# More identity transposes ahead of the weight product, later bias columns and row, and stores of z from two queues in a two-layer graph kernel

## Chip, cores and metric

The kernel runs on one core of one Trainium2 chip. The metric is device time in microseconds (us). Before the change three runs gave 1083.54, 1084.51 and 1085.01 us, so the median is 1084.51 us.

## What is computed

x has 32 batches of 512 rows and 512 columns in float32; adj is a 512 x 512 matrix: the edges of a random graph and a full diagonal, with random weights. Two layers follow each other, each with a layer norm and a relu ahead of it and a residual around it:

```python
h = jnp.maximum(_layernorm(x, axis=-1), 0.0)
x = x + einsum('nm,bmd->bnd', adj, h) @ weight + bias
h = jnp.maximum(_layernorm(x, axis=-1), 0.0)
# attention with q, k, v = h @ Wq + bq, h @ Wk + bk, h @ Wv + bv, 8 heads
scores = q @ k.T / sqrt(64) + (1.0 - adj) * -1000000000.0
x = x + softmax(scores) @ v @ Wo + bo
```

The mask term is so large that each row's softmax is one at the largest entry of its row of adj and zero elsewhere. So layer 1 is, for the inputs at hand, a gather: row n takes h of its one column, times Wv @ Wo, plus the constant row bv @ Wo + bo. A flag that the kernel computes from the data says whether this holds; then the function `single_path` runs, otherwise another that is not used here.

## The kernel before, in words

There are two stages. **The first stage**, the body of `gnn_two_layers` up to line 268, prepares what does not depend on the batch, and batch 0. It is written out in the order in which each engine shall work (a manual schedule: an engine executes its instructions in the order of the program text). On TensorE it runs, in this order:

- 14 transposes of the identity matrix (line 140), which need no loaded data, into a PSUM tile that nothing reads;
- `turn(0)`, the transposes of the first chunk of Wv (line 116), copied to `wvT` by ScalarE (line 117);
- the product Wv @ Wo (line 148) in four groups i of four matmuls; `turn(1)` to `turn(3)` stand between them, and the transposes of adj (line 106) after groups 1 and 2;
- the aggregation of batch 0 (line 225) in four groups d, with a few small matmuls between them: column counts (232), sums over partitions (218, 219), the broadcast of the row bv @ Wo (224), and the verdict of all partitions (221).

VectorE in the meantime finds the largest entry of each row of the mask (`peaks`), the layer-norm statistics (`norms`), sums of operand blocks for a seven-product scheme of 2 x 2 block multiplication (`sum_a`, `sum_b`), and then the verdict (`decide`) and the flag (line 255). The four `bias_part` steps (lines 133 and 135) form bv * Wo on VectorE, one chunk each, from the column tile `bv_c`. GpSimd computes the reciprocal standard deviations (`power`, line 326) and issues the small loads: `bv_c`, and the columns of bq and bk (`bt`), at the start (line 98), and the rows b0 and bo in the middle (line 162). ScalarE evacuates PSUM, applies the relus, and sums the squares of bq, Wq, bk and Wk (`squares`, lines 199 and 200).

Every engine then loads the flag (line 270) and branches (line 271). **The second stage**, `single_path`, runs over the batches with a table of steps: in each batch b, pieces of VectorE, ScalarE, GpSimd and DMA work are put (`put(batch, step, f)`) into 21 slots beside the 21 block products of TensorE (line 388), and batch 0 has a plain form of layer 0 (line 514). Layer 1 of a batch makes a compact z, which VectorE transposes (line 593), which is stored to DRAM by four DMAs for each part (line 598), and gathered from there back into the rows by GpSimd DMAs (`finish`, and `fetch` for the last batches, line 611). There are two parts of z in a batch: chunks 0 to 5 and chunks 6 to 10.

At the end, the batch before the last (B - 2) ends its layer 1 while batch B - 1 takes a plain form: its h rows are gathered (line 545), transposed (`transpose_all`, line 552), copied by ScalarE (553) and multiplied (`layer1_rows`, line 564), with the adds of the gathered z of batches B - 3 and B - 2 (`add_z`, line 616) and the last stores (lines 567 and 617) between the four row groups.

Of the kernel before, what the change touches and what calls it, by code (L numbers as in the profile page):

```python
# [17 lines left out]
P = 128  # L18
# [7 lines left out]
def gnn_two_layers(ctx: ExitStack, tc: tile.TileContext, x, adj, w0, b0, wq, bq, wk, bk, wv, bv, wo, bo, out):  # L26
# [15 lines left out]
    nc = tc.nc  # L42
    B, N, D = x.shape
    C = N // P
    DC = D // P
# [7 lines left out]
    adjT, yT, w0_s, sel, wvo = big("adjT"), big("yT"), big("w0_s"), big("sel"), big("wvo")  # L53
    adjT_s, w0_t, wvo_t = (keep.tile([P, 4, 2, N // 2], F32, name=n) for n in ("adjT_s", "w0_t", "wvo_t"))
    wv_s, wo_s = xs[3], xs[4]
    cvo = keep.tile([P, D], F32, name="cvo")
# [6 lines left out]
    ident = keep.tile([P, P], F32, name="ident")  # L63
# [8 lines left out]
    with ExitStack() as tmp, tc.manual_schedule():  # L72
# [6 lines left out]
        bt = [look.tile([P, DC], F32, name=f"bt{i}") for i in range(2)]  # L79
        bv_c = look.tile([P, DC], F32, name="bv_c")  # L80
# [13 lines left out]
        make_identity(nc, ident)  # L94
        nc.gpsimd.memset(ones, 1.0)
        nc.gpsimd.memset(mhalf, -0.5)
        for t, v in ((bv_c, bv), (bt[0], bq), (bt[1], bk)):
            nc.gpsimd.dma_start(t, v.rearrange("(c p) -> p c", p=P))
        first = look.tile([P, 1], F32, name="first")
        nc.scalar.activation(first, ones[:, 0:1], AF.Relu)  # L100

# [11 lines left out]
        def turn(i):  # L113
            pt = ps_l.tile([P, C, P], F32, name=f"pt{i}")
            for j in range(DC):
                nc.tensor.transpose(pt[:, j, :], wv_s[:, i, j * P:(j + 1) * P], ident)  # L116
            (nc.scalar.copy, nc.scalar.copy, nc.vector.tensor_copy, nc.vector.tensor_copy)[i](
                wvT[:, :, i * P:(i + 1) * P], pt)
# [12 lines left out]
        def bias_part(j):  # L131
            if j == 0:
                nc.vector.tensor_scalar_mul(part, wo_s[:, 0, :], bv_c[:, 0:1])
            else:
                nc.vector.scalar_tensor_tensor(part, wo_s[:, j, :], bv_c[:, j:j + 1], part, op0=ALU.mult, op1=ALU.add)

        flips = transposed(adj_s, adjT)
        idle = ps_l.tile([P, C, P], F32, name="pt3")
        for i in range(14):
            nc.tensor.transpose(idle[:, i % C, :], ident, ident)  # L140
        turn(0)
        later = {(0, 2): 1, (1, 0): 2, (1, 2): 3}
        for i in range(DC):
            ps = ps_l.tile([P, D], F32, name="mm", bufs=2)
            for j in range(DC):
                if (i, j) in later:
                    turn(later[i, j])
                nc.tensor.matmul(ps, wvT[:, j, i * P:(i + 1) * P], wo_s[:, j, :], start=(j == 0), stop=(j == DC - 1))  # L148
            if i == 0:
                for j in range(DC):  # L150
                    bias_part(j)
            if i == 1:
                next(flips)
                peaks(0)
                peaks(1)
            if i == 2:
                next(flips)
                for n in (0, 1):
                    norms[0].stats(n)
                norms[0].power()  # L160
                for v, r in ((b0, b0_r), (bo, cvo)):
                    nc.gpsimd.dma_start(r, bass.AP(tensor=v.tensor, offset=v.offset, ap=[[0, P], [1, D]]))
                norms[1].stats(0)
                norms[0].offset()
                norms[1].stats(1)
                norms[1].power()
            nc.scalar.copy(wvo[:, i, :].rearrange("p (c q e) -> p q c e", q=4, c=4),
                           ps.rearrange("p (q c e) -> p q c e", q=4, c=4))
            if i < 2:
                scale(2 * i)  # L170
                scale(2 * i + 1)
            if i == 2:
                next(flips)
                norms[0].relu(0)
                norms[0].relu(1)
                peaks(2)
                norms[1].offset()
                peaks(3)
                norms[1].relu(0)
                norms[1].relu(1)  # L180
# [8 lines left out]
        nc.vector.tensor_reduce(least, gap, AX.X, ALU.min)  # L189
        for i in range(4):  # L190
            sum_b(nc, adjT_s, adjT, i)

        sums = look.tile([P, 4], F32, name="sums")
        few = ps_l.tile([P, 4, C], F32, name="few")
# [19 lines left out]
        for d in range(DC):  # L214
            ps = ps_l.tile([P, N], F32, name="mm", bufs=2)
            for m in range(C):
                if d == 2 and m == 1:
                    nc.tensor.matmul(many[:, 0, :], ones, used, start=True, stop=True)
                    nc.tensor.matmul(many[:, 1, :], ones, sums, start=True, stop=True)
                if d == 3 and m == 2:  # L220
                    nc.tensor.matmul(few[0:1, 1, 0:1], sure, ones[:, 0:1], start=True, stop=True)
                if d == 3 and m == 0:
                    bias = ps_l.tile([P, D], F32, name="pt0")
                    nc.tensor.matmul(bias, ones, part, start=True, stop=True)
                nc.tensor.matmul(ps, hs[0][:, m, d * P:(d + 1) * P], adjT[:, m, :], start=(m == 0), stop=(m == C - 1))  # L225
            if d == 0:
                squares(0)
            nc.scalar.copy(yT[:, d, 0:N // 2 if d == 3 else N], ps[:, 0:N // 2 if d == 3 else N])
            if d == 0:
                squares(1)  # L230
                for m in range(C):
                    nc.tensor.matmul(few[:, 0, m:m + 1], both[:, m * P:(m + 1) * P], ones[:, 0:1],
                                     start=True, stop=True)
                if B > 1:
                    norms.append(Norm(nc, small, mhalf, xs[1], hs[1], range(C)))
                    norms[2].stats(0)
                nc.vector.tensor_scalar_min(used, few[:, 0, :], 1.0)
                if B > 1:
                    for c in range(1, C):
                        norms[2].stats(c)  # L240
                    norms[2].power()
                for i in range(2):
                    sum_b(nc, w0_t, w0_s, i)
                if B > 1:
                    norms[2].offset()
            if d == 2:
                decide()
                nc.vector.memset(before[:, 0:1], 0.0)
                for m in range(1, C + 1):
                    nc.vector.tensor_add(before[:, m:m + 1], before[:, m - 1:m], many[:, 0, m - 1:m])  # L250
                for c in (0, 1):
                    nc.vector.max_index(idx[:, c, :], top[:, c, :], mask[:, c, :])
                for i in range(3):
                    sum_a(nc, wvo_t, wvo, i)
        nc.vector.tensor_copy(flag, few[0:1, 1, 0:1])
        for c in (2, 3):
            nc.vector.max_index(idx[:, c, :], top[:, c, :], mask[:, c, :])
        nc.vector.tensor_copy(yT[:, 3, N // 2:N], ps[:, N // 2:N])
        nc.vector.tensor_add(cvo, bias, cvo)
        nc.vector.tensor_mul(part.rearrange("p (c q e) -> p c q e", q=4, c=4),  # L260
                             cvo.rearrange("p (q c e) -> p c q e", q=4, c=4),
                             ident.rearrange("p (q e) -> p q e", q=4).unsqueeze(1).broadcast_to([P, 4, 4, 32]))
# [33 lines left out]
def sum_b(nc, s, t, i, half=256):  # L296
    b11, b12, b21, b22 = blk(t, 0, 0, half), blk(t, 0, 1, half), blk(t, 1, 0, half), blk(t, 1, 1, half)
    if i == 0:
        nc.vector.tensor_sub(s[:, 0], b12, b11)
    elif i == 1:  # L300
        nc.vector.tensor_sub(s[:, 1], b22, s[:, 0])
    elif i == 2:
        nc.vector.tensor_sub(s[:, 2], b22, b12)
    else:
        nc.vector.tensor_sub(s[:, 3], b21, s[:, 1])
# [36 lines left out]
def single_path(ctx: ExitStack, tc: tile.TileContext, x, wv, bv, wo, bo, out, kept, room):  # L342
# [15 lines left out]
    nc = tc.nc  # L358
# [190 lines left out]
    def transpose_all(r):  # L549
        pt = ps_t.tile([P, DC, P], F32, name="pt")  # L550
        for d in range(DC):
            nc.tensor.transpose(pt[:, d, :], hs[0][:, r, d * P:(d + 1) * P], ident)
        nc.scalar.copy(hs[1][:, :, r * P:(r + 1) * P], pt)
# [35 lines left out]
    def put_z(b, s0, s1):  # L589
        if b not in Z:  # L590
            Z[b] = dram.tile([32 * S, D], F32, name="z")
            ZR[b] = work.tile([P, S, P], F32, name="hc" if b == B - 2 else "zr")
        nc.vector.transpose(ZR[b][:, s0:s1, :].rearrange("p s (c e) -> p s c e", c=4),
                            ZT[b][:, :, 32 * s0:32 * s1].rearrange("p c (s j) -> p s c j", j=32))
        rows = Z[b].rearrange("(s j) (q f) -> q j s f", j=32, q=4)
        for q in range(4):
            eng = nc.scalar if q > 1 and (b, s0) == (B - 2, 0) else nc.sync
            eng.dma_start(rows[q][:, s0:s1, :], ZR[b][32 * q:32 * q + 32, s0:s1, :])

    def finish(b):  # L600
# [39 lines left out]
    with tc.manual_schedule():  # L640
        nc.gpsimd.affine_select(out=upper, in_=ones, compare_op=ALU.is_ge, fill=0.0, base=-1,
                                pattern=[[1, P]], channel_multiplier=-1)
        for b in range(B + 1):
            todo = [[] for _ in range(21)]

            def put(batch, step, f, *args):
                if 0 <= batch < B:
                    todo[step].append(lambda: f(batch, *args))
# [58 lines left out]
                todo[3] += todo[4] + todo[5] + todo[6]  # L707
                run(layer0_rows(0), todo[0:4])
            if b == B - 1:
                put(b, 18, lambda b: transpose_all(0))  # L710
            if b == 1:
                tables = []
                put(1, 0, lambda b: tables.append(places()))
# [270 lines left out]
```

## Time and profile before

| what | value |
|---|---|
| median of three runs | 1084.51 us |
| the profiled execution: its own time | 1083.92 us |
| the profiled execution: its span | 1081.7 us |
| TensorE matmul busy | 1067.9 us (99%) |
| VectorE busy | 902.8 us (83%) |
| ScalarE busy | 362.2 us (33%) |
| GpSimd busy | 439.2 us (41%) |
| TensorE waits of over 0.3 us | 1.43 us at the start, 0.68 us at 5.66, 1.72 us at 41.86, 1.37 us at 1054.16, 8.2 us after its last matmul at 1073.5 |

PE is TensorE's matmul row, PEld its weight loads, DVE is VectorE, ACT is ScalarE, POOL is GpSimd and SP is the engine that mostly issues DMAs; a q behind an engine's name is its sequencer. Times in the timeline are microseconds from the start of the span. One row of the timeline merges consecutive instructions of one kind: start, length, what, and in square brackets the idle time before it and what ended it. A float32 matmul of 512 columns leaves two records, a transpose of 128 columns one. The last record of a row is reported longer than its distance to the next one, so starts are the better measure.

### The profile page before, as it was taken

The numbers are of one execution on the slowest core, as the hardware profiler recorded it, in microseconds if no ns is written. First come the engines' busy times: TensorE is split into PE (matmuls) and PEld (weight loads), VectorE is DVE, ScalarE is ACT, GpSimd is POOL, SyncE is SP. The second block draws the span as 40 slices with busy tenths as digits, with TensorE's granted clock in tenths as the row PEclk, the third lists the DMA queues.
The fourth block names the chain that finished last, engine by engine and source line by source line (L and its number), as shares of the span: only waits on it lengthen the run. The fifth ranks groups of instructions, "written<-read, shape, count | busy, mean of one in ns | idle before, by whom it ended". The sixth has DMA issues, their size and how long they took to land.

```text
span 1081.7 us, 15914 instructions
## 1 busy us (share of the span) xinstructions
PE 1067.9 (99%) x5418; PEld 941.9 (87%) x5418; DVE 902.8 (83%) x1851; ACT 362.2 (33%) x664; POOL 439.2 (41%) x522
## 2 busy tenths in 40 slices
PE   9999999999999999999999999999999999999996
PEld 5488989999998999998999998999898899999893
DVE  5888888888888888888888988888888888888873
ACT  5324323334422324432323432323332333442331
POOL 2024554333454333454433354433455434355413
PEclk9999999999999999999999999999999999999998
DMA  9144766667767666767666776665766666775638
GB/s 329 40 96 141 183 183 160 160 167 196 187 179 181 151 167 184 196 176 188 150 160 183 201 185 175 160 167 158 207 183 183 146 169 171 196 186 151 148 104 265
DMA packets 162443, 186.90 MB, mean 173 GB/s; under 512 B 15024, under 2 KB 102320, under 8 KB 162352
## 3 DMA queue, kind: packets, MB, share of 16 engines
q1 hardware_dynamic: 132816, 116.89, 37.2%
q0 software_dynamic: 27968, 66.61, 26.8%
q10 hardware_dynamic: 1568, 2.29, 0.6%
q8 instruction: 44, 0.72, 0.3%
q14 instruction: 47, 0.39, 0.1%
HBM read 96.28 MB, written 89.46 MB: 172 GB/s over the span
## 4 chain that ended last, share of the span: by engine, by line
PE 94%; DMA 2%; DVE 1%; POOL 1%; issue 1%; ACT 1%; SPq 0%; POOLq 0%; ACTq 0%; DVEq 0%
PE mm L388 89%; PE mm L148 1%; PE mm L225 1%; PE mm L514 1%; POOL x L602 1%; DMA yT<-z,place 0%; ACT h L337 0%; DMA h<-hs,idx 0%; DMA z<-zr 0%; DMA out_dram<-x 0%; PE pt L140 0%; DMA hs<-h 0%; PE pt L116 0%; DVE st L319 0%; DVE x L616 0%
## 5 line engine op out<-in xcount | busy, mean ns | idle before, releaser
L602 POOL DMA_INDIRECT x<-z,place x116 | 182.7, 1575 | 351.8 <-issue 193.7
L427 ACT COPY yT<-mm 128x512 f32<-128x512 f32 x124 | 71.8, 579 | 542.6 <-PE mm L388 534.6
L445 DVE TENSOR_TENSOR x<-mm,x 128x512 f32<-128x512 f32 x217 | 149.6, 689 | 86.1 <-PE mm L388 86.1
L337 ACT ACTIVATE h<-x,off,rstd 128x512 f32<-128x512 f32 x256 | 194.3, 807 | 52.2 <-DVE off L329 49.9
L326 POOL TENSOR_TENSOR rstd<-ve,mhalf 128x2 f32<-128x2 f32 (+1 forms) x97 | 106.3, 1095 | 233.5 <-DVE ve L325 233.0
L319 DVE BATCH_NORM_STATS2 st<-x 128x6 f32<-128x512 f32 x256 | 171.4, 670 | 1.2
L388 PE MATMUL mm<-adjT_s,h0s 128*128 128x256 f32 x744 | 170.8, 379 | 0.2 <-ACT yT L427 0.2
L388 PE MATMUL mm<-w_t,sel 128*128 128x256 f32 x744 | 170.7, 379 | 0.0
L388 PEld LDWEIGHTS mm<-adjT_s,h0s 128*128 128x128 f32 x744 | 141.2, 190 | 19.9 <-ACT yT L427 0.6
L388 PEld LDWEIGHTS mm<-w_t,sel 128*128 128x128 f32 x744 | 141.3, 190 | 19.3
L526 POOL DMA_INDIRECT hs<-h,dest x124 | 126.7, 1022 | 23.9 <-issue 22.4
L388 PE MATMUL mm<-w_s,yT 128*128 128x256 f32 x496 | 117.2, 379 | 0.0
L388 PE MATMUL mm<-adjT,h 128*128 128x256 f32 x496 | 117.2, 379 | 0.0
L388 PE MATMUL mm<-hTs,wvo_t 128*128 128x168 f32 x720 | 112.4, 306 | 0.0
L438 ACT ACTIVATE zs<-mm,cvo_c 128x168 f32<-128x168 f32 x240 | 83.0, 397 | 75.5 <-PE mm L388 75.5
L388 PEld LDWEIGHTS mm<-adjT,h 128*128 128x128 f32 x496 | 94.2, 190 | 13.2 <-issue 0.5
L388 PEld LDWEIGHTS mm<-hTs,wvo_t 128*128 128x128 f32 x720 | 105.5, 190 | 0.0
L388 PEld LDWEIGHTS mm<-w_s,yT 128*128 128x128 f32 x496 | 92.9, 190 | 11.3
L494 DVE TENSOR_TENSOR x<-x,b_r 128x512 f32<-128x512 f32 x124 | 83.8, 676 | 0.0
L388 PE MATMUL mm<-hT,wvo 128*128 128x168 f32 x480 | 78.2, 306 | 0.0
L388 PEld LDWEIGHTS mm<-hT,wvo 128*128 128x128 f32 x480 | 72.7, 190 | 1.6
L425 DVE TENSOR_TENSOR yT<-mm,yT 128x512 f32<-128x512 f32 x93 | 64.0, 688 | 5.7 <-PE mm L388 1.7
(159 smaller groups left out, 1285.7 us busy)
## 6 DMA issues: line engine op xcount, KB each, us to landing
out_dram<-x SPq DMA_DIRECT2D x124, 256.0 KB
x<-in_x_dram SPq DMA_DIRECT2D x120, 256.0 KB
hc<-hs SPq DMA_DIRECT2D x124, 176.0 KB
z<-zr SPq DMA_DIRECT2D x120, 96.0 KB
z<-zr SPq DMA_DIRECT2D x120, 80.0 KB
hs<-h,dest POOLq DMA_INDIRECT x124, 6.3
x<-z,place POOLq DMA_INDIRECT x116
adj_s<-in_adj_dram SPq DMA_DIRECT2D x2, 512.0 KB
```

Of the source, the lines that this page charges most:

```text
L148: nc.tensor.matmul(ps, wvT[:, j, i * P:(i + 1) * P], wo_s[:, j, :], start=(j == 0), stop=(j == DC - 1))
L319: self.nc.vector.bn_stats(st, self.src[:, self.chunks[i], :])
L326: self.nc.gpsimd.tensor_tensor(self.rstd, ve, self.mhalf[:, 0:n], ALU.pow)
L337: self.nc.scalar.activation(dst, src, AF.Relu, bias=self.off[:, i:i + 1], scale=self.rstd[:, i:i + 1])
L388: nc.tensor.matmul(bank[:, m, 0:half], lhs[:, k, m * P:(m + 1) * P], rhs[:, k, :], start=(first and m == 0 and k == 0), stop=(k == 1), ski ...
L425: nc.vector.tensor_add(dst, bank, dst)
L427: nc.scalar.copy(dst, bank)
L438: nc.scalar.activation(dst[:, m, :], bank[:, m, :], AF.Identity, bias=cvo_c[:, 2 * i + m:2 * i + m + 1])
L445: nc.vector.tensor_add(dst, bank, dst)
L494: nc.vector.tensor_add(X[b][:, c, :], X[b][:, c, :], b0_r)
L526: stored = nc.gpsimd.indirect_dma_start(out=HS[b], out_offset=bass.IndirectOffsetOnAxis(ap=dest[:, i:i + 1], axis=0), in_=H1[b][:, i, :], ...
L602: nc.gpsimd.indirect_dma_start(out=X[b][:, c, :], out_offset=None, in_=Z[b], in_offset=bass.IndirectOffsetOnAxis(ap=place[:, c:c + 1], axi ...
```

## The change

The following moves:

- 20 instead of 14 identity transposes stand ahead of `turn(0)`, and four more after it, ahead of the first matmuls of Wv @ Wo.
- The loads of `bv_c`, `bt[0]` and `bt[1]` go from the start of GpSimd's list to the place behind the two row loads, ahead of the second `power`.
- The four `bias_part` steps go from group i = 0 to the place behind the four `sum_b` of adjT.
- The whole of yT's last chunk is copied by ScalarE; VectorE had copied half of it.
- The add that makes the row `cvo` goes ahead of the last two searches for indices, right behind the flag.
- Both parts of z of batch B - 2 are stored half from SP and half from ScalarE; so far only chunks 0 to 5 were.
- `transpose_all(0)` of the last batch goes one step later.

```diff
-        for t, v in ((bv_c, bv), (bt[0], bq), (bt[1], bk)):
-            nc.gpsimd.dma_start(t, v.rearrange("(c p) -> p c", p=P))
...
-        for i in range(14):
+        for i in range(20):
             nc.tensor.transpose(idle[:, i % C, :], ident, ident)
         turn(0)
+        for i in range(4):
+            nc.tensor.transpose(idle[:, i % C, :], ident, ident)
...
-            if i == 0:
-                for j in range(DC):
-                    bias_part(j)
...
                 for v, r in ((b0, b0_r), (bo, cvo)):
                     nc.gpsimd.dma_start(r, bass.AP(tensor=v.tensor, offset=v.offset, ap=[[0, P], [1, D]]))
+                for d, r in ((bv_c, bv), (bt[0], bq), (bt[1], bk)):
+                    nc.gpsimd.dma_start(d, r.rearrange("(c p) -> p c", p=P))
                 norms[1].stats(0)
...
         for i in range(4):
             sum_b(nc, adjT_s, adjT, i)
+        for j in range(DC):
+            bias_part(j)
...
-            nc.scalar.copy(yT[:, d, 0:N // 2 if d == 3 else N], ps[:, 0:N // 2 if d == 3 else N])
+            nc.scalar.copy(yT[:, d, :], ps)
...
         nc.vector.tensor_copy(flag, few[0:1, 1, 0:1])
+        nc.vector.tensor_add(cvo, bias, cvo)
         for c in (2, 3):
             nc.vector.max_index(idx[:, c, :], top[:, c, :], mask[:, c, :])
-        nc.vector.tensor_copy(yT[:, 3, N // 2:N], ps[:, N // 2:N])
-        nc.vector.tensor_add(cvo, bias, cvo)
...
-            eng = nc.scalar if q > 1 and (b, s0) == (B - 2, 0) else nc.sync
+            eng = nc.scalar if q > 1 and b == B - 2 else nc.sync
...
-                put(b, 18, lambda b: transpose_all(0))
+                put(b, 19, lambda b: transpose_all(0))
```

## The prediction

> **What bounds the kernel now.** I read the page first, then the chain that ended last, then the timeline of each engine for the first 60 us and the last 45 us, since every edit falls there.
>
> ```profile
> span 1081.7 us, 15914 instructions
> PE 1067.9 (99%) x5418; PEld 941.9 (87%) x5418; DVE 902.8 (83%) x1851; ACT 362.2 (33%) x664; POOL 439.2 (41%) x522
> ...
> PE 94%; DMA 2%; DVE 1%; POOL 1%; issue 1%; ACT 1%; SPq 0%; POOLq 0%; ACTq 0%; DVEq 0%
> ```
>
> TensorE bounds the middle: its waits between 43.6 and 1038 us sum to under half a microsecond, and the code there is unchanged. So the change can act only ahead of 43.57, where L514 starts and after which TensorE runs on, and behind 1054, in the tail. TensorE in the prologue:
>
> ```profile
> 1.43 3.25 PE L140 MATMUL pt<-ident 128*128 128x128 f32 x14 [1.43 <-POOL ident masks.py:199]
> 4.55 1.12 PE L116 MATMUL pt<-ident,x 128*128 128x128 f32 x4
> 6.34 3.78 PE L148 MATMUL mm<-x,yT 128*128 128x512 f32 x4 [0.68 <-ACT yT L117]
> 9.91 1.05 PE L116 MATMUL pt<-ident,x 128*128 128x128 f32 x4
> 10.77 1.91 PE L148 MATMUL mm<-x,yT 128*128 128x512 f32 x4
> ...
> 43.57 7.10 PE L514 MATMUL mm<-w_s,yT 128*128 128x512 f32 x16 [1.72 <-DVE cvo L259]
> ```
>
> By starts, the first four L148 records take 3.57 us (6.34 to 9.91), later ones 1.72 (15.11 to 16.83): the clock is at half until about 10.8. At 41.86 TensorE has finished the prologue and waits 1.72 us for the add of cvo. VectorE and GpSimd:
>
> ```profile
> 8.36 0.49 DVE L133 TENSOR_SCALAR part<-x,bv_c 128x512 f32<-128x512 f32 x1 [8.36 <-DMA bv_c<-in_L_gnn_bv_dram]
> 8.88 2.33 DVE L135 SCALAR_TENSOR_TENSOR part<-x,bv_c,part 128x512 f32<-128x512 f32 x3
> ...
> 23.19 0.15 DVE L329 SCALAR_TENSOR_TENSOR off<-mv,rstd 128x2 f32<-128x2 f32 x1
> ...
> 39.98 0.15 DVE L255 CAST flag<-few 1x1 int32<-1x1 f32 x1
> ```
>
> ```profile
> 3.33 0.79 POOL L98 DMA_DIRECT2D bt<-in_L_gnn_bk_dram  x1
> ...
> 21.49 0.55 POOL L162 DMA_DIRECT2D cvo<-in_L_gnn_bo_dram  x1
> 22.24 0.71 POOL L326 TENSOR_TENSOR rstd<-ve,mhalf 128x2 f32<-128x2 f32 x1 [0.20 <-DVE ve L325]
> ```
>
> From 15.9 to the flag at 39.98 VectorE stands still only once, for 0.18 us. What is added to it there moves the flag one for one. The bias steps sit in idle time now (nothing runs on it before 8.36, nor from 11.2 to 13.15).
>
> **What the skill says.** The Trainium skill, "TensorE: Matmul & The Clock Gate", Part 1 (the HAM clock gate), has the array at half clock until one whole window of about 3.4 us, free-running, was busy. The trace agrees with a release at 10.8, one window after about 7.4; the window before that held the 0.68 us wait. The same page, Part 4 (PE-mode transpose), says that transposes do not count as busy in the same way. No row settles this: the window that released held some 0.9 us of transposes, the one that didn't held 1.1 us of them and the wait. "DMA: Bandwidth & Descriptors", Rules for kernel authors, says that a strided last dimension lowers to one descriptor per element; the column loads agree, 0.79 to 0.96 us of GpSimd against 0.55 to 0.59 for a row load of 128 times the bytes. The same page, Issuing engines are not separate DMA queues, says that issuing from two engines saves only issue time; the tail below is priced so.
>
> **Identity transposes.** Six more ahead of `turn(0)` cost 6 x 0.22 us ((4.55 - 1.43)/14) = 1.34 at half clock. The four behind it, 0.89, fill the wait for ScalarE's copy and end when it does. So L148 starts at 6.34 + 1.34 = 7.68. If the transposes count as busy, the clock is full from 7.4: four records at 0.43 end at 9.40 and `turn(1)` at 0.11 a transpose at 9.84, where before it ended at 10.77. Gain 0.93; the next group ran at full clock before. I take 1.0 us for everything led by TensorE, VectorE's start included. The loads allow this: `turn(1)`'s chunk is among the first 2 MB, and the first half of adj is needed only at 12.2.
>
> **Column loads.** They go ahead of the second `power` on GpSimd: 0.96 + 0.81 + 0.79 = 2.5 us of issue, where 0.2 us were free. The reciprocal that ended at 22.95 comes 2.3 later, and VectorE's offset at 23.19 waits in order with the last `peaks`, `both` and everything up to the flag queued behind it: 2.1 us after its 0.24 us of slack. ScalarE's third relu waits 0.35 us too, hidden, because TensorE reaches that chunk 1.7 us into L225. Landing is unknown in the new place: the row loads' packets moved only from 24.9 to 27.0, the columns stand behind them, so 27.5 to 28.5. ScalarE's squares then start about 1.5 us late; the copy of d = 0 is queued behind them, and TensorE needs its bank only at 32. Bound 0 to 0.5, taken 0. Removing the loads from the start frees nothing that is waited for.
>
> **Bias steps.** 0.49 + 2.33 us, with the overlap at the end 2.8, now in VectorE's full stretch. `used` comes at 30.2 - 1.0 + 2.1 + 2.8 = 34.1, so TensorE's count matmul (34.06 before) is just where it was: TensorE's whole lead is eaten there. `decide` no longer waits for TensorE (0.2 saved).
>
> **Row behind the flag.** The flag starts at 39.98 - 1.0 + 2.1 + 2.8 - 0.2 = 43.7 and ends at 43.83. From the flag's end to work behind the branch GpSimd took 0.72 (40.13 to 40.85, L641); TensorE's waits there add 0.2. The add of cvo ends 0.6 after the flag and needs 0.25 more (43.32 to 43.57). Both give L514 at 44.7 instead of 43.57: **+1.15 us**. ScalarE's longer copy (0.58 for 0.37) ends by 42.5, hidden by the flag. The two index searches, 1.4 us, now fall behind; VectorE comes 2.3 us late into L514's stage against TensorE's 1.15, and its idle 1.48 ahead of L464 covers that. SP's load of batch 2 is issued 3.6 us later, wanted only some 20 us on: nothing.
>
> **Tail.** The rows:
>
> ```profile
> 1055.53 0.66 PE L552 MATMUL pt<-ident,h 128*128 128x128 f32 x4 [1.37 <-DMA h<-hs,idx]
> 1056.03 1.30 PE L388 MATMUL mm<-adjT,wvo_t 128*128 128x168 f32 x8
> ```
>
> ```profile
> 1067.95 1.02 POOL L611 DMA_INDIRECT yT<-z,place x1 [5.89 <-DMA out_dram<-x]
> ```
>
> ```profile
> 1073.45 1.33 DVE L616 TENSOR_TENSOR x<-yT,x 128x512 f32<-128x512 f32 x2 [2.63 <-issue]
> ```
>
> A block product of 1.14 us (1056.03 to 1057.17) moves into the wait of 1.37 for the gather, so TensorE is 1.14 earlier behind it. SP issues six z stores from 58.92 to 61.92 now (all + 1000). With the product earlier, chunks 6 to 10 can be transposed at 55.9 and stored from 56.8 by both queues; ScalarE's last evacuation is queued behind its two issues, 0.4 late, so chunks 0 to 5 are stored from 59.4 to 60.4: 1.5 earlier than now. ScalarE's next copy of `transpose_all` then ends at 61.0, just when TensorE wants it. The gather at 67.95 is held by the landing of these stores (the named releaser, a store of rows, has nothing to give to it). The DMA engines are 70 to 99% busy from 1056 on, so the landing moves by 0 to 2. VectorE waits 2.63 for that gather and TensorE's last row ends 1.14 earlier: the end moves by 0 to -2.1, taken **-1.2**.
>
> **Sum.** Against the profiled execution: 1083.92 + 1.15 - 1.2 = 1083.9. The median of the runs stands 0.6 above it, at 1084.51; I keep that distance and forecast **1084.4**, no change. A measurement of this kernel can tell about 0.2% from no change, 2.2 us, so 1082.3 and 1086.7 are the borders. Its own range, from 0.2 to 2.0 for the prologue and 0 to -2.1 for the tail, is 1082.6 to 1086.5.
>
> **Rivals.**
> - *Slower: transposes don't release the clock.* L148 starts 1.34 late and cold. For it: Part 4 of the page, and 14 transposes that released nothing here. Against: the release at 10.8 with transposes in its window. If the window that opens at 7.4 still counts, the first group's half ends 0.7 late instead of 1.0 early, +1.7 on VectorE and the flag; if TensorE, starting at 7.68, misses that window, one more at half clock adds up to 1.7. It decides from a release later than about 9. Time 1084.4 + 1.7 to 3.4, middle **1086.9**.
> - *Faster: VectorE's chain is not what TensorE waits for*, the three issues costing little. Then L514 follows TensorE's end, 41.86 - 1.0, by the copy and 0.25: 41.75, a gain of 1.8, and with the tail 1084.51 - 3.0 = **1081.5**. Against: VectorE has no slack for 2.8 us of bias steps alone.
> - *The tail gives nothing*, its DMAs being full: 1084.51 + 1.15 = **1085.7**.
>
> **Chances.** Forecast 0.55, slower rival 0.22, faster rival 0.08, tail without gain 0.15. Faster than 1082.3: 0.06 of the faster rival and 0.03 of the forecast. Slower than 1086.7: 0.12 of the slower rival and 0.03 of the others. Range for 8 in 10: 1082.5 to 1086.8.
>
> **What would show it.** Right: first L148 near 7.6 with records of 0.43; `rstd` of the second `power` some 2 us late and VectorE idle ahead of L329; the bias steps between the sums of adjT_s and `used`; flag near 43.7, L514 near 44.7; L388 ahead of L552 and no wait of 1.37; the gather L611 near 1066.7 in the old scale. Wrong: L148 records of 0.85 up to 10.8 or later, a flag before 42, or a landing of z that didn't move.

## The result, and the profile after

The changed kernel is slower, by a little under 0.2%.

| what | before | after |
|---|---|---|
| median of 20 runs each, on the same chip | 1083.62 us | 1085.76 us |
| the profiled execution: own time | 1083.92 us | 1084.46 us |
| the profiled execution: span | 1081.7 us | 1082.6 us |

The ratio is 1.0019 [1.0011, 1.0027], which at 1084 us is +2.1 us (1.2 to 2.9). The forecast was no change. Two things are seen before any experiment: the kernel before has a median of 1083.62 over more runs, 0.9 below that of the three shown; and the profiled execution after, with 1084.46, is one of the shorter ones of its kernel.

The page of the kernel after differs little: TensorE is still busy 99% of the span, and only VectorE's share of the chain that ended last has grown.

```profile
span 1082.6 us, 15930 instructions
PE 1067.3 (99%) x5428; PEld 942.0 (87%) x5428; DVE 901.1 (83%) x1850; ACT 362.4 (33%) x664; POOL 445.6 (41%) x522
...
PE 93%; DVE 3%; POOL 1%; DMA 1%; issue 1%; ACT 0%; SPq 0%; POOLq 0%; ACTq 0%; DVEq 0%
```

TensorE's timeline of the kernel after, prologue:

```profile
1.43 4.34 PE L138 MATMUL pt<-ident 128*128 128x128 f32 x20 [1.43 <-POOL ident masks.py:199]
5.61 0.60 PE L114 MATMUL pt<-ident,x 128*128 128x128 f32 x4
6.05 0.60 PE L141 MATMUL pt<-ident 128*128 128x128 f32 x4
6.89 1.98 PE L148 MATMUL mm<-x,yT 128*128 128x512 f32 x4 [0.24 <-ACT yT L115]
8.71 0.60 PE L114 MATMUL pt<-ident,x 128*128 128x128 f32 x4
9.14 1.88 PE L148 MATMUL mm<-x,yT 128*128 128x512 f32 x4
...
33.55 0.39 PE L219 MATMUL many<-used,ones 128*128 128x4 f32 x2 [0.98 <-DVE used L238]
...
44.02 7.11 PE L514 MATMUL mm<-w_s,yT 128*128 128x512 f32 x16 [2.57 <-DVE cvo L257]
```

By starts, `turn(0)` takes 0.11 us a transpose (5.61 to 6.05) and the first L148 records 0.455 each (6.89 to 8.71): the array is at full clock from there. The clock's record has the release at 5.45, with nothing but identity transposes ahead of it. The Trainium skill, "TensorE: Matmul & The Clock Gate", Part 4 (PE-mode transpose), which says that transposes don't count as busy in the same way, does not fit these float32 ones (the records name them MATMUL and don't say whether they run in the mode that the page means). TensorE leads by 1.63 us at the second group of L148 (9.14, before 10.77), more than the 1.0 forecast. Nonetheless L514 starts at 44.02 instead of 43.57, and the wait ahead of it has grown from 1.72 to 2.57 us. VectorE in the same kernel says why:

```profile
23.66 0.16 DVE L329 SCALAR_TENSOR_TENSOR off<-mv,rstd 128x2 f32<-128x2 f32 x1 [2.02 <-POOL rstd L326]
...
29.79 0.48 DVE L131 TENSOR_SCALAR part<-x,bv_c 128x512 f32<-128x512 f32 x1
30.31 2.33 DVE L133 SCALAR_TENSOR_TENSOR part<-x,bv_c,part 128x512 f32<-128x512 f32 x3
...
42.88 0.14 DVE L256 CAST flag<-few 1x1 int32<-1x1 f32 x1
42.95 0.67 DVE L257 TENSOR_TENSOR cvo<-pt,cvo 128x512 f32<-128x512 f32 x1
```

VectorE stands still for 2.02 us ahead of L329 and then has the 2.8 us of bias steps in its full stretch. GpSimd shows what it stands still for: the second `power` is queued behind the three column loads, of which this is the last.

```profile
22.10 0.79 POOL L161 DMA_DIRECT2D bt<-in_L_gnn_bk_dram  x1
22.86 0.77 POOL L326 TENSOR_TENSOR rstd<-ve,mhalf 128x2 f32<-128x2 f32 x1
```

The tail, TensorE first:

```profile
1054.42 1.30 PE L388 MATMUL mm<-adjT,wvo_t 128*128 128x168 f32 x8
1055.75 0.66 PE L552 MATMUL pt<-ident,h 128*128 128x128 f32 x4
...
1062.06 1.98 PE L564 MATMUL mm<-wvo,h 128*128 128x512 f32 x4 [0.64 <-ACT h L553]
```

The wait of 1.37 us for the h gather is gone, as forecast, but there is a new one, of 0.64 us for ScalarE's second copy. ScalarE shows where that comes from:

```profile
1057.81 0.93 ACTq L598 DMA_DIRECT2D z<-hc  x2
1058.79 0.69 ACT L438 ACTIVATE h0s<-mm,cvo_c 128x168 f32<-128x168 f32 x2 [1.76 <-DVE hc L593]
1060.52 0.86 ACTq L598 DMA_DIRECT2D z<-hc  x2
1061.42 0.58 ACT L553 COPY h<-pt 128x512 f32<-128x512 f32 x1 [1.94 <-PE mm L564]
```

Its two issues wait for VectorE's transpose (L593) and hold up the last evacuation L438; the next two hold up the copy L553 until 1061.42. And the transpose itself starts only at 1056.93, for another reason. These are VectorE's and GpSimd's lines of the kernel after:

```profile
1056.93 0.84 DVE L593 STREAM_TRANSPOSE hc<-h0s 128x640 f32<-128x640 f32 x1 [0.59 <-POOL h0s L586]
1059.51 0.98 DVE L593 STREAM_TRANSPOSE hc<-h0s 128x768 f32<-128x768 f32 x1 [1.74 <-ACT h0s L438]
...
1076.03 0.69 DVE L616 TENSOR_TENSOR x<-yT,x 128x512 f32<-128x512 f32 x1 [0.58 <-DMA yT<-z,place]
```

```profile
1055.78 0.95 POOL L545 DMA_INDIRECT h<-hs,idx  x1 [0.30 <-PE mm L388]
1056.73 0.17 POOL L586 MEMSET h0s<- 128x64 f32 x1
...
1066.38 0.94 POOL L611 DMA_INDIRECT yT<-z,place  x1 [3.73 <-DMA z<-hc]
```

The memset that the transpose needs stands on GpSimd behind the last h gather's issue. The gather L611 of z is issued 1.57 us earlier than before (66.38 for 67.95), though TensorE comes into the tail 0.42 us later (the same block product starts at 1048.72 for 1048.30); on one scale that is 2.0 us, where 1.3 was forecast. But the last add L616, which needs it, starts at 1076.03, only 0.1 us earlier than before (1076.13), or 0.5 on that scale: from the issue of the last of the four gathers to this add it is 5.90 us (1070.13 to 1076.03), before 4.35 (1071.78 to 1076.13). From the start of L514 to the end of its last matmul TensorE takes 1029.48 us, before 1029.95: 0.47 of the 1.14 us are left.

One thing more differs, behind the last add. SP ends the program with a list of twelve waits (L979) for work that is under way. The first line is the whole list of the kernel before, the second is the fourth and the fifth wait of the kernel after, as a count, the lengths in ns and the times of the first and the last start:

```profile
L979 SPq EVENT_SEMAPHORE  x12: 28/28/28, 1078.9 to 1080.8; - x12
```

```profile
L979 SPq EVENT_SEMAPHORE  x2: 28/28/28, 1079.3 to 1081.2; - x2
```

Before, SP is through 0.14 us after the last store has landed (1080.68). After, it stands for 1.87 us ahead of the fifth wait, though what this one waits for was done before 1074, and is through 1.76 us after the last store has landed (1079.99). So the span is 0.93 us longer, although its last add is no later.

### The profile page after: what moved, and what is told of

Same layout as the page of the kernel before. It is cut to its first block, busy times and chain, and to the rows that moved or that the text cites. A ratio compares the mean times of both kernels' runs of the same rounds, so it can differ in the third digit from the quotient of the medians.

```text
span 1082.6 us, 15930 instructions
## 1 busy us (share of the span) xinstructions
PE 1067.3 (99%) x5428; PEld 942.0 (87%) x5428; DVE 901.1 (83%) x1850; ACT 362.4 (33%) x664; POOL 445.6 (41%) x522
## 3 DMA queue, kind: packets, MB, share of 16 engines
q0 software_dynamic: 27968, 66.61, 27.2%
## 4 chain that ended last, share of the span: by engine, by line
PE 93%; DVE 3%; POOL 1%; DMA 1%; issue 1%; ACT 0%; SPq 0%; POOLq 0%; ACTq 0%; DVEq 0%
PE mm L388 89%; PE mm L514 1%; PE mm L564 1%; POOL x L602 1%; DMA yT<-z,place 1%; PE mm L148 1%; DVE st L319 0%; PE pt L138 0%; POOL rstd L326 0%; DMA hc<-hs 0%; DVE x L494 0%; DVE part L133 0%; DMA z<-zr 0%; PE pt L552 0%; DVE top L126 0%
## 5 line engine op out<-in xcount | busy, mean ns | idle before, releaser
L388 PE MATMUL mm<-adjT_s,h0s 128*128 128x256 f32 x744 | 170.9, 379 | 0.1
L388 PE MATMUL mm<-w_t,sel 128*128 128x256 f32 x744 | 170.7, 379 | 0.0
L388 PEld LDWEIGHTS mm<-adjT_s,h0s 128*128 128x128 f32 x744 | 141.2, 190 | 19.8 <-ACT yT L427 0.7
L388 PEld LDWEIGHTS mm<-w_t,sel 128*128 128x128 f32 x744 | 141.3, 190 | 19.3
L526 POOL DMA_INDIRECT hs<-h,dest x124 | 132.9, 1072 | 24.0 <-issue 22.5
L388 PE MATMUL mm<-adjT,h 128*128 128x256 f32 x496 | 117.2, 379 | 0.0
L388 PE MATMUL mm<-w_s,yT 128*128 128x256 f32 x496 | 117.2, 379 | 0.0
L388 PE MATMUL mm<-hTs,wvo_t 128*128 128x168 f32 x720 | 112.4, 306 | 0.0
L438 ACT ACTIVATE zs<-mm,cvo_c 128x168 f32<-128x168 f32 x240 | 82.9, 397 | 74.5 <-PE mm L388 74.5
L388 PEld LDWEIGHTS mm<-adjT,h 128*128 128x128 f32 x496 | 94.2, 190 | 13.2 <-issue 0.5
L388 PEld LDWEIGHTS mm<-hTs,wvo_t 128*128 128x128 f32 x720 | 105.4, 190 | 0.0
L388 PEld LDWEIGHTS mm<-w_s,yT 128*128 128x128 f32 x496 | 92.9, 190 | 11.3
L388 PE MATMUL mm<-hT,wvo 128*128 128x168 f32 x480 | 78.2, 306 | 0.0
L388 PEld LDWEIGHTS mm<-hT,wvo 128*128 128x128 f32 x480 | 72.7, 190 | 1.5
```

The costliest lines, as they stand in the source:

```text
L388: nc.tensor.matmul(bank[:, m, 0:half], lhs[:, k, m * P:(m + 1) * P], rhs[:, k, :], start=(first and m == 0 and k == 0), stop=(k == 1), ski ...
L438: nc.scalar.activation(dst[:, m, :], bank[:, m, :], AF.Identity, bias=cvo_c[:, 2 * i + m:2 * i + m + 1])
L526: stored = nc.gpsimd.indirect_dma_start(out=HS[b], out_offset=bass.IndirectOffsetOnAxis(ap=dest[:, i:i + 1], axis=0), in_=H1[b][:, i, :], ...
```

## The experiments

Each was timed next to the kernel before on the same chip: `e1` to `e4` on one chip, `e5` to `e8` on a second and `e9` to `e12` on a third; us are the ratio times 1084. Edits are given against the kernel before, unless it says "to the kernel after".

**The two halves.** `e1_prologue` has all of the change but its last two lines, `e2_tail` has only those two:

```diff
-            eng = nc.scalar if q > 1 and (b, s0) == (B - 2, 0) else nc.sync
+            eng = nc.scalar if q > 1 and b == B - 2 else nc.sync
...
-                put(b, 18, lambda b: transpose_all(0))
+                put(b, 19, lambda b: transpose_all(0))
```

> Only the edits of the prologue (identity transposes, column loads, bias steps, row behind the flag, whole copy); the tail is as before. Theory A (VectorE's longer chain to the flag holds the lead back, and is most of the loss): slower by 1.0 to 2.0 us, the flag at 43 to 44 us, L514 at 44.0 to 44.9 against 43.57 before. Theory B (the loss lies in the tail, where ScalarE's queue got longer): within 0.5 us of before. Theory C (the many identity transposes upset the TensorE clock later on): slower by 1 to 3 us, with a second stretch at half clock in the record.

Measured: 1086.08 us (22 runs) against 1084.51 (59), 1.0011 [1.0003, 1.0020], or +1.2 us. L514 starts at 44.15 after a wait of 2.57. Its trace has no second stretch at half clock ahead of the end of the program; theory C is taken up below.

> Only the edits of the tail (z of batch B - 2 from two queues in both parts, first transposes of the last batch one step later); the prologue is as before. Theory A: between no change and a gain of 1 us. Theory B: slower by 0.5 to 1.5 us, with TensorE waiting some 0.6 us for the second copy L553, whose start is held by four DMA issues of ScalarE, and the gather L611 earlier by about 1.5 us without an earlier end. Theory C: no change.

Measured: 1084.91 us, 1.0006 [0.9997, 1.0014], +0.65 us (-0.3 to 1.5). By itself that is no difference that could be told, but a gain of 1.2 us lies outside the interval. Together the halves make 1.85 of the 2.1 us. TensorE's line has the new wait here too, and ScalarE's has both of its causes:

```profile
1060.30 1.98 PE L564 MATMUL mm<-wvo,h 128*128 128x512 f32 x4 [0.57 <-ACT h L553]
```

```profile
1057.03 0.69 ACT L438 ACTIVATE h0s<-mm,cvo_c 128x168 f32<-128x168 f32 x2 [1.69 <-DVE hc L593]
...
1059.66 0.59 ACT L553 COPY h<-pt 128x512 f32<-128x512 f32 x1 [1.94 <-DVE hc L593]
```

**The transposes alone**, 20 + 4 in place of 14 (`e3_idents`):

```diff
-        for i in range(14):
+        for i in range(20):
             nc.tensor.transpose(idle[:, i % C, :], ident, ident)
         turn(0)
+        for i in range(4):
+            nc.tensor.transpose(idle[:, i % C, :], ident, ident)
```

> Only the identity transposes, 20 and 4 in place of 14. Theory A: faster by 0.7 to 1.6 us, since VectorE's chain now follows TensorE's lead up to the flag, and L514 starts near 42.5. Theory C: not faster, or slower by 1 us and more. Theory B says nothing of it (about the same as A).

Measured: 1084.31 us, 0.9995 [0.9987, 1.0004], -0.5 us, which is less than expected and cannot be told from none. L148 starts at 6.66 and L514 at 42.04. Here the traces of other kernels with the old start help: the clock was released at 10.82 in the profiled execution before, but at 5.12 in that of `e2_tail` and at 9.86 in that of `e4_later`, and L514 started at 43.57, 42.24 and 43.08. In the ten further traces with the new start the release came between 4.17 and 7.34. As far as these traces tell, the transposes replace a release that is early or late by one that is always early, so that the lead is gained in some runs only, and the profiled execution before happened to be a late one. The traces also show what differs: with 14 transposes TensorE works from 1.43 to 5.66 us and then waits for 0.68, and in the kernel before and in `e4_later` the clock stayed at half in the stretch of 3.41 us that held this wait; with 20 and 4 the wait is 0.24 in the kernel after.

**The later step alone** (`e4_later`): `put(b, 19, ...)` for `put(b, 18, ...)`, stores as before.

> Only the first transposes of the last batch one step later. Theory A and B: TensorE's wait of 1.37 us near 1054 goes and it ends about 1.1 us earlier; the gather L611 of the last z moves by about the 1.1 us by which the product is earlier, if the memset L586 and the copies don't hold it, so a gain of 0.3 to 1.2 us. If the end hangs on the DMA engines' load alone: no change within 0.5 us.

Measured: 1083.01 us, 0.9985 [0.9978, 0.9992], **-1.6 us**. So the step does give its 1.14 us and a little more, and there is no wait for L553:

```profile
1054.77 0.66 PE L552 MATMUL pt<-ident,h 128*128 128x128 f32 x4 [0.23 <-DMA h<-hs,idx]
...
1058.56 3.60 PE L564 MATMUL mm<-wvo,h 128*128 128x512 f32 x8
```

By difference, the two queues then cost `e2_tail` 2.2 us (1.9 by the two medians).

**The row and the bias steps.** `e5_ident_row` has the transposes, the row right behind the flag and ScalarE's full copy; `e6_bias_only` has the late bias steps as well, with the column loads still at the start. The edit in both:

```diff
-            nc.scalar.copy(yT[:, d, 0:N // 2 if d == 3 else N], ps[:, 0:N // 2 if d == 3 else N])
+            nc.scalar.copy(yT[:, d, :], ps)
...
         nc.vector.tensor_copy(flag, few[0:1, 1, 0:1])
+        nc.vector.tensor_add(cvo, bias, cvo)
...
-        nc.vector.tensor_copy(yT[:, 3, N // 2:N], ps[:, N // 2:N])
-        nc.vector.tensor_add(cvo, bias, cvo)
```

> Identity transposes and the row behind the flag with the whole copy by ScalarE; column loads, bias steps and tail as before. Theory A (VectorE's added work holds the flag, and only that): L514 follows TensorE's end by the copy, near 41.2 us where the transposes alone gave 42.04, so faster than before by 1.0 to 2.0 us. Rival (the row behind the flag gains nothing because the branch has the same length as the wait for the add): like the transposes alone, 0 to 0.7 us faster.

> The prologue's edits with the column loads left at the start: of what VectorE got, only the 2.8 us of bias steps. Theory A: the flag near 40.8 us with VectorE not idle ahead of L329, L514 near 41.9 (2.1 earlier than with the loads moved), so 0.3 to 1.5 us faster than before. Rival (the bias steps alone eat the whole lead): L514 at 43 or later, within 0.5 us of before.

Measured: `e5_ident_row` 1082.86 us, 0.9993 [0.9985, 1.0001], -0.8 us; `e6_bias_only` 1083.76 us, 0.9997 [0.9989, 1.0006], -0.3 us. Neither time can be told from none, so theory A's gain is not shown by them, but the traces are plain. Without bias steps and loads L514 starts at 40.96 after a wait of only 0.72, named for ScalarE's copy. With the bias steps the flag is at 40.92, L514 at 42.06 and the wait is 1.68. So the loads, which are all that is left, are the other 2.0 us of flag and L514 (42.88 and 44.02 in the kernel after).

**The two queues undone in the kernel after** (`e7_after_sp`), and **only ScalarE's issues for chunks 6 to 10 put behind its last evacuation** (`e8_after_defer`, to the kernel after):

```diff
+        for f in held:
+            f()
+        held.clear()
...
+            if eng is nc.scalar and s0:
+                held.append(lambda q=q: nc.scalar.dma_start(rows[q][:, s0:s1, :], ZR[b][32 * q:32 * q + 32, s0:s1, :]))
+            else:
+                eng.dma_start(rows[q][:, s0:s1, :], ZR[b][32 * q:32 * q + 32, s0:s1, :])
```

> The changed kernel with one edit undone: chunks 6 to 10 of the last z are stored by SP alone. Theory B2 (the two DMA issues put on ScalarE cost some 2 us, everything else sums to a small gain): 0 to 1 us faster than before, no wait of TensorE for L553 of the second row group. Rival (the loss is all in the prologue, and the comparison of the tail edits was noise): slower by 1.0 to 2.5 us, as the changed kernel.

> The changed kernel with ScalarE's two issues of chunks 6 to 10 moved behind its last evacuation L438. If the harm of the two issues is that they hold that evacuation (and with it the transposes and stores of chunks 0 to 5): 0 to 1 us faster than before. If it is that they hold the second copy L553, ahead of which all four issues still stand: slower by 1 to 2.5 us as the changed kernel, with TensorE's wait for L553 kept.

Measured: 1085.83 us, 1.0015 [1.0006, 1.0023], and 1085.08 us, 1.0015 [1.0007, 1.0023]. Both are +1.6, against +2.1 for the kernel after, and both lie in the slower of the ranges expected: the waits for L553 are shorter in the traces (0.29 and 0.25), and the time does not follow as far as `e4_later` and `e2_tail` would have it. So ScalarE's hold on L438 and L553 is seen in the traces, but a price for it in time is not shown; and the queues are not the whole loss, something else differs from run to run. `e8_after_defer`'s trace shows it. TensorE's line:

```profile
44.60 8.58 PE L514 MATMUL mm<-w_s,yT 128*128 128x512 f32 x16 [2.56 <-DVE cvo L257]
```

The row takes 8.58 us, in the kernel after 7.11. Here are the stretches around it; the columns are the stretch in us, its length, the busy time of TensorE's matmuls, its weight loads, VectorE, ScalarE and GpSimd with the count of instructions, and then the granted clock, the DMA share and GB/s.

```profile
40.00:44.10 4.10, 2.04 (x7) 0.70 (x6) 4.03 (x11) 2.02 (x4) 0.00 (x0) 1.00 0.00 0
44.20:47.50 3.30, 2.90 (x4) 1.38 (x5) 3.27 (x9) 1.29 (x2) 0.29 (x1) 0.50 0.68 202
47.60:51.00 3.40, 3.40 (x9) 1.49 (x9) 3.40 (x7) 0.00 (x0) 0.00 (x0) 1.00 0.28 105
```

The clock is **0.50** from 44.17 to 47.58, one stretch of 3.41 us, and full again after it. L388 starts 15.73 us behind L514 (44.60 to 60.33), in the kernel after 14.25 (44.02 to 58.27): the price is 1.5 us. TensorE stood idle for 2.13 us of the stretch ahead of the fall (40.76 to 44.17). In the kernel after's own profiled execution, and in those of `e1_prologue` and `e7_after_sp`, the wait of 2.57 lay across two such stretches with at most 1.67 in one, and the clock did not fall; nor did it in `e10_after_behind` with 1.79. All stretches at full clock in the 14 traces last a whole number of 3.413 us, counted from the release, which came between 4.17 and 10.82 us. So it falls or not with where the wait lies against a period of 3.41 us, and that differs from run to run. The Trainium skill, "TensorE: Matmul & The Clock Gate", Part 1 (the HAM clock gate), puts the throttled state after a whole idle window; here 2.13 idle us of 3.41 were enough.

The clock of every run fits this, with a reservation. One half-clock stretch of 3.41 us in 1083 lowers a run's mean by 0.0016. But the mean also holds the stretch at half clock behind the last matmul, 5.4 us of the span in the trace after and 7.8 in that of `e4_later`, whose mean is 0.996 with no fall ahead of it; and a run that ends late has more of it. So 0.996 proves no fall, and 0.995 is the better sign. Of the 153 runs of the kernel before beside the experiments, nine had a mean of 0.996 and none less; of the 20 runs after, four had 0.995 and two 0.996. These six average 1087.5 us and the other fourteen 1085.5; weighed with 6 in 20 that is 0.6 us, an estimate from above.

**The wait filled** (`e9_after_fill`, to the kernel after): 20 more identity transposes at the end of TensorE's prologue, so that it works while it waits for the flag.

```diff
+        spare = ps_l.tile([P, C, P], F32, name="pt1")
+        for i in range(20):
+            nc.tensor.transpose(spare[:, i % C, :], ident, ident)
         nc.vector.tensor_copy(flag, few[0:1, 1, 0:1])
```

> The changed kernel with 20 more identity transposes (some 2.2 us, their result unused) at the end of TensorE's prologue, in its wait for the flag. Theory D (the wait, grown from 1.72 to 2.57 us, makes the clock fall to half for one window of 3.4 us in a part of the runs, which costs 1.7 us each time): L514 starts as in the changed kernel, near 44.0 to 44.6, but no run has a mean clock of 0.995, and the ratio to before falls from 1.0019 to about 1.0010 to 1.0014. Rival (the clock is no cause): the ratio stays at 1.0019 or above, and low clocks stay.

Measured: 1084.91 us (22 runs) against 1083.82 (50), 1.0011 [1.0004, 1.0018], +1.2 us: 0.9 less than the kernel after, although L514 starts 0.6 later in its trace.

```profile
41.90 2.35 PE L258 MATMUL pt<-ident 128*128 128x128 f32 x20
44.63 5.82 PE L517 MATMUL mm<-w_s,yT 128*128 128x512 f32 x13 [0.38 <-PE pt L258]
```

None of its 22 runs has a mean clock below 0.997. That count, against six of 20 (four of them at 0.995), is the stronger evidence; the two ratios' intervals overlap.

**The column loads behind the second `power`** (`e10_after_behind`, to the kernel after):

```diff
-                for d, r in ((bv_c, bv), (bt[0], bq), (bt[1], bk)):
-                    nc.gpsimd.dma_start(d, r.rearrange("(c p) -> p c", p=P))
                 norms[1].stats(0)
...
                 norms[1].power()
+                for d, r in ((bv_c, bv), (bt[0], bq), (bt[1], bk)):
+                    nc.gpsimd.dma_start(d, r.rearrange("(c p) -> p c", p=P))
```

> The changed kernel with the three column loads behind the second power on GpSimd instead of ahead of it. Theory A: VectorE doesn't wait ahead of the second L329, the flag comes 2.0 us earlier, near 41 us, L514 near 42.1 with a wait of about 1.7 us, and no fall of the clock; faster than the changed kernel by 2 us or a little more, so within 0.8 us of before. Rival (the load's place costs nothing, the bias steps are all): as the changed kernel, slower than before by 1.2 us or more.

Measured: 1084.81 us, 1.0007 [0.9999, 1.0016], +0.76 us. VectorE no longer stands still ahead of L329; the flag comes at 41.72, 1.16 earlier, and L514 at 42.86. TensorE started later in this trace (L148 at 7.49 for 6.89), and VectorE with it (first copy at 12.11 for 11.50); from that copy on the flag takes 29.61 us instead of 31.38, so that 1.8 of the 2.0 us are back. The wait is still 2.05 us, and ten of 14 runs have a clock of 0.996 or less, three of them 0.995. So the 2 us that were expected against the kernel after are 1.3, and the low clocks, which were not expected, are there.

**The parts that pay, together.** `e11_best_later` is `e5_ident_row` with the later step: neither the loads, nor the bias steps, nor the queues are moved. `e12_best_queues` adds the two queues.

> Identity transposes, the row behind the flag, and the first transposes of the last batch one step later; column loads, bias steps and the stores of z as before. If the parts add up: -0.8 (transposes and row) and -1.6 (later step), so 1.6 to 3.0 us faster than before. If the later step's gain was an accident of the measurement: 0.3 to 1.2 us faster.

> As e11, but with the changed kernel's stores of z from two queues too. Theory B2 (the two issues on ScalarE cost 1 to 2 us): slower than e11 by 1 to 2.5 us, with TensorE's wait of some 0.6 us for L553. Rival (the queues cost nothing): within 0.7 us of e11.

Measured: `e11_best_later` **1080.67 us** (7 runs), 0.9970 [0.9957, 0.9983], -3.25 us; `e12_best_queues` 1081.79 us (20), 0.9981 [0.9972, 0.9990], -2.1. The first beats both kernels. The lines are its start of the plain layer 0 (L515 in its text), and then the second row group of the last batch in the other:

```profile
41.01 7.10 PE L515 MATMUL mm<-w_s,yT 128*128 128x512 f32 x16 [0.72 <-ACT yT L230]
```

```profile
1059.18 1.98 PE L565 MATMUL mm<-wvo,h 128*128 128x512 f32 x4 [0.20 <-ACT h L554]
```

`e11_best_later` has no wait of TensorE in the tail. The two queues add the 0.20, and the gather of z comes 1021.79 us behind L514 instead of 1020.55: 1.2 us later, not earlier. The times agree with that, but their intervals overlap. The three prices for the queues (2.2 from `e2_tail` and `e4_later`, 1.2 here, 0.45 in the kernel after, each uncertain by about 1 us) do not settle one number; none shows a gain.

The traces give the queues a price of their own. All six with both parts stored from two queues (the kernel after, `e2_tail`, `e8_after_defer`, `e9_after_fill`, `e10_after_behind`, `e12_best_queues`) have SP's stop of 1.8 to 2.2 us ahead of its fifth last wait, and none of the other eight has it. From the landing of the last store to the end of the span it is 1.0 to 1.45 us in these eight, and 2.3 to 2.7 in five of the six (1.54 in `e10_after_behind`): some 1.3 us, in `e8_after_defer` too, where ScalarE's issues were put off. What SP stops for is not shown; its program has two instructions fewer in all six (1015 for 1017). No run keeps the queues without the stop, so its share in the three prices is read from traces alone.

## Why the prediction was wrong

The forecast was a sum of +1.15 for the prologue and -1.2 for the tail. The first came out in size, in part by luck; the second is the step that failed.

1. **Identity transposes, "1.0 us for everything led by TensorE".** The mechanism was right: release at 5.45 (7.4 was reckoned with), a lead of 1.63 in the trace. What failed is that it was counted against one execution with a release at 10.82. The same text had earlier ones in `e2_tail` and `e4_later`, and the transposes alone measured -0.5 us (-1.4 to +0.4).
2. **Column loads, 2.1 us of stall.** It measured 2.02; the columns of bq landed at 27.2 (27.5 forecast). Moving the loads behind the second `power` took 1.8 of it back.
3. **Bias steps, 2.8 us in VectorE's full stretch.** Right (29.79 to 32.6), and TensorE's lead was eaten at the count matmul, by the 0.98 us wait at 33.55.
4. **Row behind the flag, L514 at 44.7.** With the lead of 1.63 in place of 1.0 that is 44.07; it was 44.02. `e1_prologue` measured +1.2 us where the sum had +1.15.
5. **A term that the sum lacked: the clock in the longer wait.** The prediction priced the wait ahead of L514 as time alone. It grew from 1.72 to 2.57 us, and in some runs the clock then falls to half for 3.41 us. `e8_after_defer`'s trace shows it at 1.5 us; `e9_after_fill` puts its mean at 0.9, the runs' clocks at 0.6 or less. It is inside `e1_prologue`'s +1.2 (four of its 22 runs have a clock of 0.995), so that the late flag itself cost less than forecast. That the sum comes out at +1.15 is in part luck: the lead was 0.6 us greater than forecast, while the clock was left out, the starting point was a late execution, and the trace of `e1_prologue` has a wait that is 1.0 us longer than in the kernel after (below).
6. **Tail, "the end moves by 0 to -2.1, taken -1.2".** This is the step that failed, and that turned the sign: it measured +0.65 (-0.3 to 1.5), 1.85 us off. The block product moved into the gather's wait is worth more than forecast (`e4_later`: -1.6). The two queues, priced as stores "1.5 earlier than now", cost some 2 us in its place. For one, "ScalarE's next copy of `transpose_all` then ends at 61.0, just when TensorE wants it" failed: it ended at about 1062, since the first transpose L593 waited for a memset that stands behind the h gathers on GpSimd, ScalarE's issues waited for L593, L438 for the issues, the second L593 for L438, and the copy L553 for the next issues. The prediction gave 0.4 us to the first link on ScalarE and nothing to GpSimd. For another, the gather moved by 2.0 (forecast 1.3) but took 1.5 us longer to land, and the last add moved by 0.5, not by up to 2.1. And the prediction put nothing for what SP does behind the last store, where the traces with two queues lose some 1.3 us. Which of these makes up the time is not shown by an experiment: `e8_after_defer` has most of the first undone, keeps the last, and is no faster beyond the noise.

The rivals: that the transposes don't release the clock is wrong, and that VectorE's chain isn't waited for is too. "The tail gives nothing", 1085.7, has the time of the 20 runs, but it reached it from a base 0.9 too high; against the same runs the change costs 2.1, not 1.15.

What stays open: why undoing the queues gains so little in the kernel after; what SP stops for; and whether the clock falls in the six slower runs after exactly where it does in `e8_after_defer`, since only one execution of each kernel has a trace. A wait of TensorE at about 101 us, ahead of L388, is 0.26 us in ten of the 14 traces and 1.28 in the other four (`e1_prologue`, `e3_idents`, `e5_ident_row`, `e7_after_sp`); all four have the new transposes, but so have seven of the ten. It follows from one GpSimd instruction, here in the kernel after and then in `e1_prologue`:

```profile
97.91 1.41 POOL L326 TENSOR_TENSOR rstd<-ve,mhalf 128x4 f32<-128x4 f32 x1 [5.76 <-DVE ve L325]
```

```profile
98.04 3.21 POOL L326 TENSOR_TENSOR rstd<-ve,mhalf 128x4 f32<-128x4 f32 x1 [5.76 <-DVE ve L325]
```

The reciprocal takes 3.21 us in the four and 1.41 in the ten, and VectorE and then TensorE wait for it. Why it does, and whether that belongs to a kernel or to an execution, no run shows. If it belongs to the kernel, 1.0 us in the times of these four is not their edits' own: that would fit `e11_best_later`, which has no such wait and is 0.85 us better than `e5_ident_row` and `e4_later` together, and it would raise the queues' price in the kernel after from 0.45 to about 1.5.

## What to carry to other kernels

A DMA issue takes its place in the list of the engine that issues it, and waits there for its data: before moving one, name the small operations behind it, and who needs them (here a reciprocal behind three column loads, an evacuation behind two stores, a memset behind four gathers). Read a tail to the end of the span and not only to its last add: here 1 us of the loss lies behind it. A wait of TensorE can have a second price, the clock; here it was bought off with work that needs no data (`e9_after_fill`), and it is better not to lengthen the wait. Test the parts of a change singly: here the transposes, the row and the later step together made the kernel 3.25 us faster, and with the loads, the bias steps and the queues added it was 2.1 slower.

## What was not expected of the hardware

- Float32 transposes of the identity alone release the clock: at 5.45 us, with 4 us of them and nothing else.
- The clock can fall after 2.13 idle us in a stretch of 3.41, and is back one stretch later; 1.79 idle us did not bring it down.
- With the same kernel text ahead of them, the clock was released at 5.12, 9.86 or 10.82 us in three traces with 14 transposes; with 20 and 4 of them it was released by 7.34 in all eleven.
- An instruction of one kind and size on GpSimd took 1.41 us in ten traces and 3.21 in four, at the same place of the program.
- With two issues fewer in its list, SP stopped for 1.8 to 2.2 us at the end of the program, in six traces of six, ahead of a wait whose condition had been met.
